# A two-layer graph kernel: the score and value stages of a head pair joined into one stage of 16 steps each, and all adjacency quarters read from memory

## The chip, the core and the metric

The kernel runs on one core of one Trainium2 chip. The metric is the device time of one launch in microseconds (us), as the median of several runs. Everything is computed in 32-bit floats. The engines of the core work side by side, each through its own queue in order: PE (TensorE, matrix products), ACT (ScalarE), DVE (VectorE), POOL (GpSimd), and SP, which here issues nearly all DMA transfers.

## What is computed

There are 16 batch items of 1024 nodes with 256 channels, and one adjacency matrix of 1024 x 1024. Cut to what matters:

```python
# layer 0, on each batch item
c = mean over channels of x                                   # one value per node
A = abs(abs(sigmoid(c_m - c_n) - 0.5) - 0.5) * 2              # 1024 x 1024, symmetric
g = relu((x^T @ (adj * A)) * para)                            # the queries
k, v = split(x @ kv_w)                                        # keys and values, 4 heads of 64
attn = softmax(q @ k^T * scale);  x = layernorm(x + attn @ v)
# layer 1
h = relu(x @ w1_loop + adj @ (x @ w1_neigh) + b1)             # 128 wide
h = relu(h @ w2_loop + adj @ (h @ w2_neigh) + b2)             # 256 wide
x = layernorm(x + (x + h) * 0.5)
```

## The kernel before

All instructions are written out by hand in program order (`tc.manual_schedule()`), and each engine works through its own instructions in that order. The main loop in `run()` goes over the 16 batch items `b`. In iteration `b` the attention of item `b` is computed, the queries, keys and values of item `b + 1` are prepared, and layer 1 of earlier items is done: the first graph product of item `b - 1` (`c1`) and the second of item `b - 2` (`c2`) are joined in `Joined.run`. These two products with the adjacency matrix, of two quarters by two quarters each, are done with seven products of half size instead of eight (`Joined.product`, numbers 1 to 7, in the order 1, 2, 6, 7, 5, 4, 3). Each product reads one half-size matrix: the quarters themselves for 1, 2 and 3, and sums of quarters for 6, 7, 5 and 4. Three quarters (`half_adj`) stay on chip as constants; the fourth and the four sums lie in DRAM (`far_adj`), and `Joined.fetch` reads them as two tiles of 512 KB each.

The attention is done in four units: two head pairs, and for each two halves of 512 queries. `Attention.scores(u)` (L626 to L640) has 8 steps, one per 128 keys. In each, PE computes the scores of both heads of the pair into a PSUM tile of two banks (tag "big", 3 buffers), ACT takes the exponential of 128 x 1024 values (L629), and DVE adds it to a running sum (L633, L635); at the end DVE turns and reduces the sum. `Attention.outputs(u)` (L648, L653) multiplies the values with the 8 exponentials into a PSUM tile of one bank (tag "bank", 2 buffers), and DVE turns the result. `Attention.add` divides and adds into the item's residual.

Between the units stand the functions `gap0` to `gap2`:

- `gap0`, after the value steps of unit 0: `means` sums the channels of the next item on ACT (L262), POOL scales the sums (L263), and SP writes the 1024 values to DRAM (`line`, L265), from where they are read back into all 128 partitions (`c_row`, L270). Between the writing and the reading back SP issues `c2.load_x` (L748) and the transfers of two adjacency sums (L183).
- `gap1`, after unit 1: `c1.inner` (L755), the joined product (L762, L939) with pieces of the next item's queries between its parts, and before it the transfers of two rows of `adj` (L474) and of the other two adjacency sums.
- `gap2`, after unit 2: the end of layer 1 for `c2` (`last`, L823, L825, with the residual on DVE).

After unit 3 follow the queries (L577), the layer norm (`BlockedNorm`) and the keys and values (`KeysValues`) of the next item. Most tiles in SBUF are "row" tiles of 128 x 1024 values (4 KB per partition), 25 buffers shared by all uses; a new tile waits until the one that had its buffer has been used up. A DMA that waits for a buffer or for data holds back all later ones on SP.

In item 0 there is no layer 1 yet, and in item 1 there is only the first product of item 0, done with all eight parts (`GraphConv.first`). Behind the loop the last items are brought to an end.

Of the kernel before, what the change touches and what calls it, by code (L numbers as in the profile page):

```python
# [18 lines left out]
def kernel(  # L19
# [31 lines left out]
    nc = tc.nc  # L51
# [17 lines left out]
    ROWS = 25  # L69
# [95 lines left out]
    for a in range(1, Q):  # L165
# [7 lines left out]
    half_adj = {(0, 0): const.tile([P, TJ, FB], F32, name="adjT_00"),  # L173
                (1, 0): const.tile([P, TJ, FB], F32, name="adjT_10"),
                (1, 1): const.tile([P, TJ, FB], F32, name="adjT_11")}
    far_adj = {n: dram.tile([2, P, N], F32, tag=f"adj_{n}", name=f"adjT_{n}", bufs=1) for n in ("01", 1, 2, 3, 4)}
# [16 lines left out]
    def adj_block(i, j, k, rows01):  # L193
        return of_rows(rows01, k) if (i, j) == (0, 1) else half_adj[i, j][:, k, :]

    def adj_sums(rows01, k):

        w11, w21, w22 = (half_adj[ij][:, k, :] for ij in ((0, 0), (1, 0), (1, 1)))
        w12 = of_rows(rows01, k)
# [404 lines left out]
    class Attention:  # L604
# [6 lines left out]
        def __init__(self, b, xB, qT, kT, v):  # L611
            self.b, self.xB, self.qT, self.kT, self.v = b, xB, qT, kT, v
            self.parts, self.o = {}, {}

            self.rden = small.tile([P, len(UNITS) * FB // S], F32, tag="rden", name=f"rden_{b}", bufs=2)
            self.sums = small.tile([P, NC, NB], F32, tag="sums", name=f"sums_{b}", bufs=2)

        def scores(self, u):

            b, (pair, j) = self.b, UNITS[u]  # L620
            self.pr = []
            for mt in range(NT):
                ps = big_psum(f"s_{b}_{u}_{mt}")
                for s in range(2):
                    rows = slice(s * HD, (s + 1) * HD)
                    nc.tensor.matmul(ps[:, ts(s, FB)], self.kT[rows, pair, ts(mt, P)], self.qT[rows, pair, ts(j, FB)],  # L626
                                     start=True, stop=True)
                pr = row_tile(f"pr_{b}_{u}_{mt}")
                nc.scalar.activation(pr, ps, AF.Exp)  # L629
                self.pr.append(pr)  # L630
                if mt == 1:
                    acc = row_tile(f"acc_{b}_{u}")
                    nc.vector.tensor_add(acc, self.pr[0], pr)  # L633
# [9 lines left out]
        def outputs(self, u):  # L643
            b, (pair, j) = self.b, UNITS[u]
            pav = bank_psum(f"av_{b}_{u}")
            for mt in range(NT):
                for s in range(2):
                    nc.tensor.matmul(pav[s * HD:(s + 1) * HD, :],  # L648
                                     self.v[:, mt, pair * P + s * HD:pair * P + (s + 1) * HD],
                                     self.pr[mt][:, ts(s, FB)], start=(mt == 0), stop=(mt == NT - 1))  # L650
            name = f"o_{b}_{u}"
# [88 lines left out]
    class GraphConv:  # L740
# [29 lines left out]
        def first(self, rows01, between=None):  # L770
            for j in range(NJ):
                ph = half_psum(f"h1_ps_{self.b}_{j}")
                self.loop(ph, j, start=True)
                for mt in range(NT):
                    if (j, mt) == (0, TJ) and between:
                        between()
                    nc.tensor.matmul(ph, self.t1[:, mt, :], adj_block(mt // TJ, j, mt % TJ, rows01),
# [26 lines left out]
        def neighbours(self, j, pu, mts, rows01):  # L804
            for mt in mts:
                nc.tensor.matmul(pu, self.h1[:, ts(mt, P)], adj_block(mt // TJ, j, mt % TJ, rows01),
                                 start=(mt == 0), stop=(mt == NT - 1))

        def second(self, rows01, between=None):

            self.uT = row_tile(f"uT_{self.b}")
            for j in range(NJ):
                pu = half_psum(f"u_ps_{self.b}_{j}")
                self.neighbours(j, pu, range(TJ), rows01)
                if j and between:
                    between()
                self.neighbours(j, pu, range(TJ, NT), rows01)
# [42 lines left out]
        def ending(self, dst, rows01, aside):  # L860
# [40 lines left out]
            self.second(rows01, lambda: (bias(0), bias(1), aside(), bias(2), bias(3), quarter(0)))  # L901
# [5 lines left out]
    class Joined:  # L907
# [27 lines left out]
        def product(self, n, dst, start=False, again=False):  # L935
            w = {1: (0, 0), 2: (1, 0), 3: (1, 1)}.get(n)
            rows = None if w else self.far.pop({4: 4, 5: 1, 6: 2, 7: 3}[n])
            for k in range(TJ):
                nc.tensor.matmul(dst, self.x[n][:, k, :], half_adj[w][:, k, :] if w else of_rows(rows, k),  # L939
# [40 lines left out]
    def run():  # L980
# [32 lines left out]
        rows01 = []  # L1013

        def turn_adj(mts):
            for mt in mts:
                i, k = mt // TJ, mt % TJ
                src = tiles.pop(mt)
                for j in range(NJ):
                    if (i, j, k % 2) == (0, 1, 0):  # L1020
                        rows01.append(row_tile(f"adjT_01_{k // 2}"))
                    nc.vector.transpose(adj_block(i, j, k, rows01), src[:, ts(j, FB)])

        for t in range(NT):
# [3 lines left out]
            if t == 4:  # L1028
# [4 lines left out]
                adj_sums(rows01, 0)  # L1033
# [4 lines left out]
        for b in range(B):  # L1038
# [6 lines left out]
            if c2 and more:  # L1045
                c2.load_h1()

# [5 lines left out]
            def gap0():  # L1053
                row = means(q, xb, str(b + 1))
                if both:
                    c2.load_x()
                    both.fetch(2, 3)
                row()
                ready["xT"] = channel_major(blocked, f"xT_{b + 1}")

# [5 lines left out]
            def gap1():  # L1066
# [3 lines left out]
                if both:  # L1070
                    both.left(nc.gpsimd)
                    both.fetch(1, 4)
                    both.run({1: (lambda: q.left(nc.gpsimd),),
                              2: (lambda: att.add(0, 1),),
                              6: (lambda: q.likeness(0), lambda: c3 and c3.moments()),
                              7: (lambda: q.likeness(TJ),),
                              5: (weigh_first,),
                              4: (lambda: c3 and c3.finish(out[b - 3]),),
                              3: (c1.turn_blocks,)})
                else:  # L1080
                    q.left(nc.gpsimd)
                    for t in (0, TJ):
                        q.likeness(t)
                    store("01", rows01)
                    c1.first(rows01, lambda: (att.add(1), adj_sums(rows01, 1), adj_sums(rows01, 2), weigh_first()))
                    c1.turn_blocks()

            def gap2():
                if both:
                    c2.last()  # L1090
# [185 lines left out]
```

## Time and profile before

| | |
|---|---|
| median of 3 runs | 2150.01 us (2149.88 to 2150.26) |
| profiled execution | span 2148.2 us, 1.8 us under the median |
| granted TensorE clock, mean | 0.998 |
| PE busy | 2136.2 us, 99% |
| DVE busy | 1906.8 us, 89% |
| ACT busy | 1039.8 us, 48% |
| POOL busy | 355.2 us, 17% |
| DMA | 290.73 MB, mean 135 GB/s, queue q1 busy 55.6% of 16 engines' span |
| one iteration (item 7 to item 8, first score to first score) | 924.02 to 1056.17, 132.15 us |

The profile is one execution, not the one that was timed. Busy shares are averages over the span. The ends of matmuls are modelled, so that a busy share of PE says little by itself: the distance from the start of one matmul to the start of the next says more. In a timeline each line merges neighbouring instructions of one kind, with its start, its length and their number (x32: 32 instructions; a 32-bit matmul of 512 columns counts as two). In the DMA queue's timeline the length is the time that SP took to issue, and not the time to landing.

### The profile page before, as it was taken

To read this page: it belongs to the slowest core of one execution; us is meant where nothing else is said; L and a number is where in the kernel's file an instruction comes from. 1 tells how busy PE (TensorE), PEld (TensorE's weight loads), DVE (VectorE), ACT (ScalarE), POOL (GpSimd) and SP (SyncE) were. 2 spreads that over 40 slices of the span, in tenths; PEclk is the share of its full clock that TensorE was granted. 3 is DMA by queue.
4 is the path that set the end of the run, shared out by engine and by line. 5 is a ranking of instruction groups with operands and counts; after the bars stand their busy time and mean duration, and the time that the engine had idled before them with its cause. 6 is when DMAs were issued, how large, how long until landed. Compare 5 with 4: busy or idle time off the path is not lost.

```text
span 2148.2 us, 23745 instructions
## 1 busy us (share of the span) xinstructions
PE 2136.2 (99%) x8360; PEld 1021.5 (48%) x8360; DVE 1906.8 (89%) x2350; ACT 1039.8 (48%) x1374; POOL 355.2 (17%) x201
## 2 busy tenths in 40 slices
PE   9999999999999999999999999999999999999998
PEld 5344444544445444454445444454445444444354
DVE  5999988899999899989999899999999899999964
ACT  5745545545345454445544555345553445545412
POOL 1011120121302113030130301203012130121021
PEclk9999999999999999999999999999999999999999
DMA  9393653736557375573755637565374664744343
GB/s 238 117 147 118 147 157 110 146 117 133 149 137 164 95 134 155 137 172 88 122 163 134 160 89 120 173 128 157 109 115 159 128 157 120 129 134 95 122 137 100
DMA packets 612207, 290.73 MB, mean 135 GB/s; under 512 B 504816, under 2 KB 569712, under 8 KB 612080
## 3 DMA queue, kind: packets, MB, share of 16 engines
q1 hardware_dynamic: 611808, 288.87, 55.6%
q8 instruction: 68, 1.11, 0.2%
q14 instruction: 59, 0.48, 0.1%
q10 hardware_dynamic: 272, 0.26, 0.0%
HBM read 242.35 MB, written 46.72 MB: 135 GB/s over the span
## 4 chain that ended last, share of the span: by engine, by line


## 5 line engine op out<-in xcount | busy, mean ns | idle before, releaser
L629 ACT ACTIVATE pr<-s 128x1024 f32<-128x1024 f32 x512 | 476.1, 1054 | 223.2 <-PE s L626 222.6
L635 DVE TENSOR_TENSOR acc<-acc,pr 128x1024 f32<-128x1024 f32 x384 | 482.9, 1258 | 42.2 <-DVE acc L635 2.8
L626 PE MATMUL s<-qT,kT 64*128 64x512 f32 x2048 | 456.8, 596 | 0.0
L648 PE MATMUL av<-pr,v 128*64 128x512 f32 x2048 | 453.6, 595 | 0.0
L626 PEld LDWEIGHTS s<-qT,kT 64*128 64x128 f32 x2048 | 191.6, 186 | 246.3 <-ACT pr L629 112.8
L648 PEld LDWEIGHTS av<-pr,v 128*64 128x64 f32 x2048 | 141.4, 137 | 298.6 <-issue 283.0
L328 POOL TENSOR_TENSOR rstd<-rstd,neg_half 128x32 f32<-128x32 f32 x16 | 98.9, 6181 | 1102.5 <-DVE rstd L326 1102.5
L490 ACT ACTIVATE wg<-c_row,c_col 128x1024 f32<-128x1024 f32 x128 | 146.1, 1141 | 73.9 <-DVE accB L637 65.7
L496 DVE SCALAR_TENSOR_TENSOR wg<-wg,adj 128x1024 f32<-128x1024 f32 x128 | 150.0, 1210 | 11.9 <-ACT wg L491 11.9
L939 PE MATMUL hu_ps<-adj,R 128*128 128x512 f32 x360 | 158.0, 595 | 0.0
L491 ACT ACTIVATE wg<-wg 128x1024 f32<-128x1024 f32 x128 | 135.3, 1057 | 4.1
L577 PE MATMUL g_ps<-wg,S 128*128 128x512 f32 x224 | 115.5, 597 | 0.0
L577 PE MATMUL g_ps<-T,S 128*128 128x512 f32 x224 | 115.2, 596 | 0.0
L577 PE MATMUL g_ps<-wg,x 128*128 128x512 f32 x224 | 109.0, 599 | 0.0
L939 PE MATMUL hu_ps<-adjT,t 128*128 128x512 f32 x240 | 105.7, 592 | 0.0
L939 PEld LDWEIGHTS hu_ps<-adj,R 128*128 128x128 f32 x360 | 67.3, 190 | 78.9 <-issue 76.3
L633 DVE TENSOR_TENSOR acc<-pr,pr 128x1024 f32<-128x1024 f32 x64 | 77.0, 1203 | 19.7 <-ACT pr L629 19.7
L586 ACT COPY P<-g_ps 128x512 f32<-128x512 f32 x14 | 8.2, 585 | 174.8 <-PE g_ps L577 174.8
L758 ACT COPY t<-t_ps 128x1024 f32<-128x1024 f32 x16 | 16.2, 1013 | 143.9 <-PE t_ps L755 143.9
L637 DVE STREAM_TRANSPOSE accB<-acc 128x1024 f32<-128x1024 f32 x64 | 79.7, 1246 | 2.2
L640 DVE TENSOR_REDUCE den_part<-accB 128x32 f32<-128x1024 f32 x64 | 78.0, 1220 | 2.2
L823 PE MATMUL h_ps<-w2n_sb,uT 128*128 128x256 f32 x240 | 72.7, 385 | 0.0
(204 smaller groups left out, 3022.0 us busy)
## 6 DMA issues: line engine op xcount, KB each, us to landing
adj<-in_adj_dram SPq DMA_DIRECT2D x128, 512.0 KB, 5.1
adj<-adjT SPq DMA_DIRECT2D x120, 512.0 KB, 10.2
para<-in_L_gnn_para_dram SPq DMA_DIRECT2D x32, 512.0 KB, 4.4
xB_a<-in_x_dram SPq DMA_DIRECT2D x128, 128.0 KB, 4.0
x1d<-xB_a SPq DMA_DIRECT2D x128, 128.0 KB, 3.4
x<-x1d SPq DMA_DIRECT2D x16, 1024.0 KB, 16.1
xB<-in_x_dram SPq DMA_DIRECT2D x120, 128.0 KB, 4.4
x<-in_x_dram SPq DMA_DIRECT2D x15, 1024.0 KB, 6.9
```

What stands on the lines that cost most here:

```text
L328: nc.gpsimd.tensor_tensor(self.rstd, self.rstd, neg_half, ALU.pow)
L490: nc.scalar.activation(wg, self.c_row, AF.Abs, bias=self.c_col[:, t:t + 1], scale=-1.0)
L491: nc.scalar.activation(wg, wg, AF.Tanh, scale=-0.5)
L496: nc.vector.scalar_tensor_tensor(wg, wg, 1.0, self.adj.pop(t), op0=ALU.add, op1=ALU.mult)
L577: nc.tensor.matmul(self.p[n], x_n[:, k, :], w_n, start=(k == 0), stop=(k == TJ - 1))
L626: nc.tensor.matmul(ps[:, ts(s, FB)], self.kT[rows, pair, ts(mt, P)], self.qT[rows, pair, ts(j, FB)], start=True, stop=True)
L629: nc.scalar.activation(pr, ps, AF.Exp)
L635: nc.vector.tensor_add(acc, acc, pr)
L637: nc.vector.transpose(accB, acc)
L640: nc.vector.tensor_reduce(self.part[:, u % 2, :], by_node(accB), AX.X, ALU.add)
L648: nc.tensor.matmul(pav[s * HD:(s + 1) * HD, :], self.v[:, mt, pair * P + s * HD:pair * P + (s + 1) * HD], self.pr[mt][:, ts(s, FB)], start ...
L939: nc.tensor.matmul(dst, self.x[n][:, k, :], half_adj[w][:, k, :] if w else of_rows(rows, k), start=(start and k == 0), stop=(k == TJ - 1), ...
```

## The change

It does five things.

1. **Score and value stages.** For b from 2 on, `both_scores(pair)` computes the scores of both query halves of a pair in one go, 16 steps, and `two_units(pair)` then the 16 value steps. Every fourth step (2, 6, 10, 14) uses two one-bank PSUM tiles instead of a big one, and two Exps of half size. The first unit's values go to half of a big PSUM tile, the second unit's to a bank tile; DVE's turning of them (`turn`) is a function of its own, and comes in DVE's order behind all 16 sums of the stage.
2. **Order of the pieces.** `means` and what hangs on it now stand behind `both_scores(0)`, `c2.last()` stands directly behind the joined product, `c1.turn_blocks()` behind that, and the six later rows of `adj` and their weights behind `both_scores(1)`.
3. **Adjacency quarters.** `half_adj` is gone. All four quarters are stored to DRAM in iteration 1, and the three that the joined product uses are read in each joined product, as "00", "10" and "11".
4. **Order of the transfers.** "00" and "10" stand directly behind `line`, then `c2.load_x`, `c_row`, the two rows of `adj`, and 2, 3, 1, 4 and "11".
5. **Row tiles.** 31 buffers instead of 25.

Items 0 and 1 keep their stages of 8 steps. `rows01` becomes `quarters` throughout. The diff, cut to this:

```diff
-    ROWS = 25
+    ROWS = 31
...
-    half_adj = {(0, 0): const.tile([P, TJ, FB], F32, name="adjT_00"),
-                (1, 0): const.tile([P, TJ, FB], F32, name="adjT_10"),
-                (1, 1): const.tile([P, TJ, FB], F32, name="adjT_11")}
-    far_adj = {n: dram.tile([2, P, N], F32, tag=f"adj_{n}", name=f"adjT_{n}", bufs=1) for n in ("01", 1, 2, 3, 4)}
+    QUARTERS = {(0, 0): "00", (0, 1): "01", (1, 0): "10", (1, 1): "11"}
+    far_adj = {n: dram.tile([2, P, N], F32, tag=f"adj_{n}", name=f"adjT_{n}", bufs=1)
...
+    def fetch_quarters(name, ready=None):
+        return {ij: (ready or {}).get(n) or fetch(n, name) for ij, n in QUARTERS.items()}
+
+    def adj_block(i, j, k, quarters):
+        return of_rows(quarters[i, j], k)
+
...
-        def scores(self, u):
+        def scores(self, u, first=None):
 
             b, (pair, j) = self.b, UNITS[u]
-            self.pr = []
+            self.pr[u] = prs = []
             for mt in range(NT):
-                ps = big_psum(f"s_{b}_{u}_{mt}")
+                name = f"s_{b}_{u}_{mt}"
+                split = first is not None and (first + mt) % 4 == 2
+                if split:
+                    halves = [bank_psum(f"{name}_{s}") for s in range(2)]
+                else:
+                    ps = big_psum(name)
+                    halves = [ps[:, ts(s, FB)] for s in range(2)]
                 for s in range(2):
                     rows = slice(s * HD, (s + 1) * HD)
-                    nc.tensor.matmul(ps[:, ts(s, FB)], self.kT[rows, pair, ts(mt, P)], self.qT[rows, pair, ts(j, FB)],
+                    nc.tensor.matmul(halves[s], self.kT[rows, pair, ts(mt, P)], self.qT[rows, pair, ts(j, FB)],
                                      start=True, stop=True)
                 pr = row_tile(f"pr_{b}_{u}_{mt}")
-                nc.scalar.activation(pr, ps, AF.Exp)
-                self.pr.append(pr)
+                if split:
+                    for s in range(2):
+                        nc.scalar.activation(pr[:, ts(s, FB)], halves[s], AF.Exp)
+                else:
+                    nc.scalar.activation(pr, ps, AF.Exp)
+                prs.append(pr)
                 if mt == 1:
                     acc = row_tile(f"acc_{b}_{u}")
-                    nc.vector.tensor_add(acc, self.pr[0], pr)
+                    nc.vector.tensor_add(acc, prs[0], pr)
                 elif mt > 1:
                     nc.vector.tensor_add(acc, acc, pr)
...
+        def both_scores(self, pair):
+            for j in range(NJ):
+                self.scores(NJ * pair + j, j * NT)
+
+        def outputs(self, u, psum_tile=bank_psum, turned=True):
             b, (pair, j) = self.b, UNITS[u]
-            pav = bank_psum(f"av_{b}_{u}")
+            pav = psum_tile(f"av_{b}_{u}")
+            prs = self.pr.pop(u)
             for mt in range(NT):
                 for s in range(2):
                     nc.tensor.matmul(pav[s * HD:(s + 1) * HD, :],
                                      self.v[:, mt, pair * P + s * HD:pair * P + (s + 1) * HD],
-                                     self.pr[mt][:, ts(s, FB)], start=(mt == 0), stop=(mt == NT - 1))
-            name = f"o_{b}_{u}"
+                                     prs[mt][:, ts(s, FB)], start=(mt == 0), stop=(mt == NT - 1))
+            self.o[u] = pav
+            if turned:
+                self.turn(u)
+
+        def turn(self, u):
+            name, pav = f"o_{self.b}_{u}", self.o[u]
             self.o[u] = work.tile([P, FB], F32, tag="o", name=name) if u % 2 else row_tile(name)[:, 0:FB]
             nc.vector.transpose(self.o[u], pav)
...
-            w = {1: (0, 0), 2: (1, 0), 3: (1, 1)}.get(n)
-            rows = None if w else self.far.pop({4: 4, 5: 1, 6: 2, 7: 3}[n])
+            rows = self.far[{1: "00", 2: "10", 3: "11", 4: 4, 5: 1, 6: 2, 7: 3}[n]]
             for k in range(TJ):
-                nc.tensor.matmul(dst, self.x[n][:, k, :], half_adj[w][:, k, :] if w else of_rows(rows, k),
+                nc.tensor.matmul(dst, self.x[n][:, k, :], of_rows(rows, k),
                                  start=(start and k == 0), stop=(k == TJ - 1), skip_group_check=again)
...
-            if c2 and more:
+            if c2:
                 c2.load_h1()
+            if more:
+                q = (FastQueries if c1 else Queries)(b + 1, xb)
 
             def load_next():
                 nonlocal coming
                 if b + 2 < B:
                     coming = load_x(b + 2, str(b + 2)), load_blocked(b + 2, str(b + 2))
 
...
             def weigh_first():
                 q.times_adj(0)
                 q.times_adj(TJ)
                 q.right(0)
 
+            def two_units(pair, before_first=lambda: None, before_second=lambda: None):
+                u = NJ * pair
+                att.outputs(u, half_psum, turned=False)
+                before_first()
+                att.turn(u)
+                att.outputs(u + 1, turned=False)
+                before_second()
+                att.turn(u + 1)
+
...
+            elif more:
+                att.both_scores(0)
+                row = means(q, xb, str(b + 1))
+                both.fetch("00", "10")
+                c2.load_x()
+                row()
+
+                def next_xT():
+                    ready["xT"] = channel_major(blocked, f"xT_{b + 1}")
+
+                two_units(0, before_second=next_xT)
+                kv = KeysValues(b + 1, ready["xT"])
+                kv.sums()
+                for t in (0, TJ):
+                    q.load(t)
+                both.fetch(2, 3, 1, 4, "11")
+                c1.inner()
+                both.left(nc.gpsimd)
+                both.run({1: (lambda: q.left(nc.gpsimd),),
+                          2: (lambda: att.add(0, 1),),
+                          6: (lambda: q.likeness(0), lambda: c3 and c3.moments()),
+                          7: (lambda: q.likeness(TJ),),
+                          5: (weigh_first,),
+                          4: (lambda: c3 and c3.finish(out[b - 3]),)})
+                c2.last()
+                c1.turn_blocks()
+                att.both_scores(1)
+                order = (1, TJ + 1, 2, TJ + 2, 3, TJ + 3)
+                for t in order:
+                    q.load(t)
+                for t in order:
+                    q.likeness(t)
+
+                def weigh_second():
+                    q.times_adj(1)
+                    q.times_adj(TJ + 1)
                     q.right(1)
...
+
+                two_units(1, before_second=weigh_second)
+            else:
+                att.both_scores(0)
+                two_units(0)
+                att.add(0, 1)
+                att.both_scores(1)
+                two_units(1)
...
-                c2.load_h1()
                 c2.load_x()
-                both.fetch(2, 3)
+                both.fetch("00", "10", 2, 3)
                 c1.inner()
                 both.left(nc.gpsimd)
-                both.fetch(1, 4)
-                both.run({1: (lambda: att.add(3), att.watch), 2: (norm.mean, norm.squares, norm.sum_squares), 7: (norm.variance,),
+                both.fetch(1, 4, "11")
+                both.run({1: (lambda: att.add(2, 3), att.watch), 2: (norm.mean, norm.squares, norm.sum_squares), 7: (norm.variance,),
...
-        both.fetch(2, 3, 1, 4)
-        rows01 = fetch("01", "e")
+        both.fetch("00", "10", 2, 3, 1, 4, "11")
+        quarters = fetch_quarters("e", both.far)
```

## Prediction

> **What bounds the kernel now.** I read the busy shares first, then TensorE's timeline over one steady iteration, then ScalarE's and the DMA queue's timelines over the same stretch, then busy times by stretch. The chain of waits is empty on this page, so the bound has to be read from the start times of the matmuls.
>
> The page's busy shares:
>
> ```profile
> PE 2136.2 (99%) x8360; PEld 1021.5 (48%) x8360; DVE 1906.8 (89%) x2350; ACT 1039.8 (48%) x1374; POOL 355.2 (17%) x201
> ```
>
> TensorE's timeline (start us, us, what):
>
> ```profile
> 924.02 7.14 PE L626 MATMUL s<-qT,kT 64*128 64x512 f32 x32
> 931.09 7.09 PE L648 MATMUL av<-pr,v 128*64 128x512 f32 x32
> 938.11 7.14 PE L626 MATMUL s<-qT,kT 64*128 64x512 f32 x32
> 945.17 7.09 PE L648 MATMUL av<-pr,v 128*64 128x512 f32 x32
> 952.19 3.84 PE L755 MATMUL t_ps<-w1n_sb,x1T 128*128 128x128 f32 x32
> 955.87 1.88 PE L762 MATMUL hu_ps<-x1T,w1l_sb 128*128 128x512 f32 x4
> 957.58 7.03 PE L939 MATMUL hu_ps<-adjT,t 128*128 128x512 f32 x16
> 964.45 0.33 PE L662 MATMUL den_ps<-den_part,fold 128*128 128x64 f32 x2
> 964.62 10.52 PE L939 MATMUL hu_ps<-adj,R 128*128 128x512 f32 x24
> ```
>
> 16 matmul rows of 512 columns take 964.45 - 957.58 = 6.87 us, 0.429 us each. A score or value stage is 16 such passes (two 64-wide matmuls side by side), so 6.87 us too; it takes 7.07 and 7.02 us from start to start. Nothing else is lost: TensorE never waits for data here, it pays 0.20 us per score stage and 0.15 us per value stage for changing the tiling of its array. Scores of this batch item start at 924.02, the next item's at 1056.17: 132.15 us per item, all of it matmul time. So the end moves one for one with anything that makes TensorE wait.
>
> **What is removed.** Per joined iteration (b = 2 to 14, 13 of them) four score and four value stages become two and two: 2 x 0.20 + 2 x 0.15 = 0.70 us. The second layer (L823, L825) no longer stands between a value and a score stage: it takes 1004.84 - 997.74 = 7.10 us for 16 pairs spaced 0.43 us (6.9 us), so 0.20 us more. Together 0.90 us; b = 15 saves 0.70. Sum: 13 x 0.90 + 0.7 = **12.4 us gained**, if TensorE stays fed.
>
> **What feeds the score stage.** A score step is 0.86 us on TensorE; ScalarE's Exp is one per 0.92 us (8 in 7.44 us). Steps 2, 6, 10, 14 use the two bank tiles, so every step reuses the buffer of four steps earlier. Exp 11 ends at about 925.20 + 11 x 0.92 + 1.05 = 936.4; step 15 starts at 924.2 + 15 x 0.86 = 937.1: 0.7 us to spare. Two half Exps cost 2 x 0.48 us (L455 to L457, 923.01 to 923.48) against 0.92, or up to 2 x 0.585 (the mean of L586's copies of this shape): 0 to 1.0 us per stage, hidden by that spare up to its 0.7. I take 0. The first value tile now sits in a big buffer that the joined product's third accumulator takes next: VectorE turns it after 16 sums, two transposes and two reductions (2 x 11.6 us from 929.54, so at 953.5); TensorE wants it at 955.5. 2 us to spare, no cost.
>
> **What is moved: the row of means and all transfers behind it.** The means are queued on ScalarE behind 8 Exps today, behind 16 then.
>
> ```profile
> 925.20 7.44 ACT L629 ACTIVATE pr<-s 128x1024 f32<-128x1024 f32 x8 [1.12 <-PE s L626]
> 932.44 0.49 ACT L262 ACTIVATE x<-x 128x256 f32<-128x256 f32 x1
> ...
> 939.28 7.44 ACT L629 ACTIVATE pr<-s 128x1024 f32<-128x1024 f32 x8 [3.50 <-PE s L626]
> ```
>
> They begin at 932.44; then at 925.20 + 12 x 0.92 + 4 x 0.95 = 940.0, 7.5 us later. The DMA of "line" needs them (POOL's c_col), and SP is in order:
>
> ```profile
> 936.17 0.38 SPq L265 DMA_DIRECT2D line<-c_col  x1
> 936.60 0.57 SPq L748 DMA_DIRECT2D x<-x1d  x1
> 937.23 11.02 SPq L183 DMA_DIRECT2D adj<-adjT  x4
> 948.35 0.58 SPq L270 DMA_DIRECT2D c_row<-line  x1
> 949.03 1.06 SPq L474 DMA_DIRECT2D adj<-in_adj_dram  x2
> 952.38 4.16 SPq L183 DMA_DIRECT2D adj<-adjT  x4
> ```
>
> So line goes out at 943.7 instead of 936.17, and everything behind it. What line does to the queue, by stretches (us, busy of PE, PEld, DVE, ACT, POOL, clock, DMA share, GB/s):
>
> ```profile
> 936.00:940.00 4.00, 4.00 (x22) 1.39 (x19) 3.74 (x4) 0.72 (x1) 0.14 (x1) 1.00 0.73 133
> 940.00:948.00 8.00, 8.00 (x40) 3.10 (x38) 7.77 (x7) 6.72 (x8) 2.10 (x1) 1.00 0.54 38
> 948.00:966.00 18.00, 18.00 (x78) 9.46 (x75) 14.53 (x15) 1.60 (x2) 8.70 (x6) 1.00 0.91 356
> ```
>
> After its 1024 writes of 4 bytes almost nothing moves for some 10 us (38 GB/s), then the backlog drains, one 512 KB tile per 1.28 us (time to landing of the tiles of L183). The same read of x, issued with no line ahead in the last iteration, lands in 6.6 us; here in 16.1.
>
> Today the first half of far tile "2", which product 6 reads at 964.62, is issued at 937.23 and lands 16.4 us later, at 953.6: 11 us early. In the change, between line and that tile stand "00" and "10" (4 tiles), x (2 tiles' bytes), c_row, two adjacency rows: 9 tiles' bytes, then it. Today x, four tiles, c_row, two rows, then the first half of "1" are the same bytes in the same queue; that half was issued at 952.38 and landed 11.1 us later, at 963.5: 27.3 us after line. Over the 13 iterations this lies between 26.3 and 29.6. So "2" would land at 943.7 + 27.3 = 971.0. TensorE wants it at 964.62 less the 0.35 us saved on two stages: 964.3. **A wait of 6.7 us**, with product 6 and the whole rest of TensorE's queue behind it. What could shorten it: during the stoppage about 300 packets of 1 KB went through; packets of 4 KB could carry 0.9 MB more, 2.2 us at 410 GB/s. What stopped longest decides a landing, so I take half: 5.6 us; bounds 4.5 and 9 (29.6 us after line). The other tiles follow at 1.28 us, faster than TensorE uses them (1.72 us per tile). "00" (wanted at 957.2) and "10" (960.7) come out of the same queue at about 956 to 960: no further wait.
>
> **After the wait: the array's clock.** At the program's start, out of idleness:
>
> ```profile
> 1.41 3.61 PE L990 MATMUL idle<-ident 128*128 128x128 f32 x16 [1.41 <-POOL ident masks.py:199]
> 4.86 2.60 PE L232 MATMUL xT_ps<-ident,x 128*128 128x128 f32 x16
> ```
>
> 16 transposes take 3.45 us, 0.215 us each; the next 16 of the same shape come at 0.15 us or less ((7.30 - 4.86) / 16). Half speed for 3.45 us is 1.7 us lost. No stretch of this trace shows whether a pause of 6 us brings it back: bounds 0 and 3.4 us per pause (twice that row); I take that row, 1.7. [...] By the rows alone it could also be nothing, which would make the sum 22 us lower.
>
> **The rest.** In the second stage VectorE starts its sums later, behind the second layer's residuals; I put pair(3)'s third difference at 0 to 0.3 us after its product wants it: 0 to 4 us in all, I take 0. Extra bytes: 3 MB in 15 joined products, 45 on 291 MB, in stretches where the queue is idle (966 to 984 moves 1 GB/s): nothing but what is counted. Six extra row tiles replace 24 KB of constant tiles.
>
> **The sum.** 13 x (5.6 + 1.7) = 94.9 us lost, 12.4 gained: 82.5 us. The profiled run spans 2148.2 us, 1.8 under the median; added to the median, 2150.0 + 82.5 = 2232.5, so **2232 us**.
>
> **Rivals.**
> 1. *The streams come in time* (faster): if "2" lands within 20.6 us of line, 13 x 0.90 + 0.7 is all there is: 2137.6 us. For it: today's "2" lands 17.4 us after line. Against it: seven tiles' bytes more stand ahead then. It decides at a landing of 20.6 us; every 1 us beyond is 13 us, so a wait of 0.95 us already eats the gain. 0.18.
> 2. *The wait without a slow clock*: 2150 - 12.4 + 13 x 4.5 to 6.7 = 2196 to 2225. 0.26.
> 3. *Long packets slip through the stoppage, so 1 to 3 us are left*: 2150 - 12.4 + 13 to 39 = 2151 to 2177. 0.10.
> 4. *The change does not do what it says*: scores still come in eights because of buffers taken back late. Then stages still follow each other without a switch, and only ScalarE's lag shows: about no change. 0.04.
>
> **How the numbers follow.** The forecast has 0.42; its own range is 2196 to 2277 (13 x (7.0 + 3.4 + 0.3) - 12.4 = 127 above). Slower by over 0.2% (about what a measurement of this kernel can tell from no change, 4.3 us): 0.42 + 0.26 + 0.10 = 0.78; within it 0.04; faster 0.18. The range for 8 in 10 leaves out rival 1 alone: 2150 to 2277.
>
> **What would show it.** Right: in each of 13 iterations one gap on TensorE of 4 to 9 us before L939's first "adj,R" product, ended by DMA adj<-adjT; line issued some 19.7 us after the item's first score; "2" landing 24 to 30 us after line; matmuls after the gap spaced 0.86 us for a while; six switches of tiling per item. Wrong: no gap there and 131.25 us per item (rival 1), or a gap that ends at ScalarE's Exp or VectorE's turning instead.

## The result, and the profile after

The changed kernel takes 2256.2 us (2255.96 to 2259.01) against 2150.0 us: a ratio of 1.0497, 95% interval 1.0482 to 1.0511. It is 106 us slower; the forecast was 82 us slower, 2232 us, with 2277 as the upper end. The profiled execution spans 2254.2 us, 106.0 us more than the one of before.

The busy shares of the page, and the groups of products, with the idle time before them after the bar:

```profile
PE 2160.5 (96%) x8356; PEld 1038.2 (46%) x8356; DVE 1895.1 (84%) x2346; ACT 1046.6 (46%) x1486; POOL 342.0 (15%) x201
...
L959 PE MATMUL hu_ps<-adj,R 128*128 128x512 f32 x480 | 239.9, 658 | 66.3 <-DMA adj<-adjT 66.3
```

TensorE was 99% busy and is 96% busy now, and nearly all of its new idle time stands before one line. L959 is what L939 was. TensorE's timeline over the item that starts at 963.11 us shows where:

```profile
963.11 14.00 PE L633 MATMUL s<-qT,kT 64*128 64x512 f32 x64
977.04 13.95 PE L664 MATMUL av<-pr,v 128*64 128x512 f32 x64
...
997.91 7.10 PE L959 MATMUL hu_ps<-adj,t 128*128 128x512 f32 x16 [1.43 <-DVE K L387]
1004.85 0.33 PE L683 MATMUL den_ps<-den_part,fold 128*128 128x64 f32 x2
1010.85 11.32 PE L959 MATMUL hu_ps<-adj,R 128*128 128x512 f32 x19 [5.67 <-DMA adj<-adjT]
```

The two joined stages run without a gap: 977.04 - 963.11 = 13.93 us for 32 passes of 0.429 (13.74), and 13.88 us for the value stage. Then there are two gaps. Product 1 starts 34.8 us after the item's first score instead of 33.2 (in this item the profile puts the wait down to VectorE's K; the first half of "00" landed at 997.77, 0.14 us before the start, so I read it as that transfer). Product 6 starts only when the first half of "2" is there. Its 19 passes shown take 11.32 us, where 24 took 10.52 before.

The DMA queue's timeline over the same item:

```profile
983.37 0.38 SPq L266 DMA_DIRECT2D line<-c_col  x1
983.80 2.00 SPq L182 DMA_DIRECT2D adj<-adjT  x4
985.85 0.73 SPq L769 DMA_DIRECT2D x<-x1d  x1
995.52 2.53 SPq L271 DMA_DIRECT2D c_row<-line  x1
998.15 1.29 SPq L475 DMA_DIRECT2D adj<-in_adj_dram  x2
999.58 11.52 SPq L182 DMA_DIRECT2D adj<-adjT  x9
```

The order is the one of the diff, and c_row goes out only when line has landed. The stretches behind line (us, busy of PE, PEld, DVE, ACT, POOL, clock, DMA share, GB/s) repeat the stoppage and the backlog of before:

```profile
983.00:987.00 4.00, 4.00 (x22) 1.33 (x20) 3.69 (x4) 0.00 (x0) 0.35 (x1) 1.00 0.12 1
987.00:995.00 8.00, 8.00 (x53) 4.98 (x50) 7.72 (x8) 0.20 (x1) 1.99 (x1) 1.00 0.25 27
995.00:1012.00 17.00, 9.90 (x24) 4.38 (x23) 14.38 (x21) 1.40 (x2) 10.33 (x7) 0.94 1.00 375
```

27 GB/s while line's writes run, 375 GB/s afterwards; and a granted clock of 0.94 in the stretch that holds the pause. TensorE's waits over the whole run (us in total, times, longest), where before had none beyond the 1.4 us at the program's start:

```profile
PE hu_ps L959 <- DMA adj<-adjT: 75.9, 24, 5.7
...
PE sum_ps L253 <- DVE rden_min L702: 1.9, 1, 1.9
PE den_ps L683 <- DVE den_part L651: 1.5, 1, 1.5
```

From the start times of the matmuls, summed over the 13 joined items (each term is what the distance between two starts exceeds its usual value by):

| | per item | in all |
|---|---|---|
| product 1 waits for "00" | 0.6 to 1.6 us | 14.5 |
| product 6 waits for the first half of "2" | 4.83 to 5.83 us | 68.4 |
| passes at half speed behind that pause, 0.854 us apart | 1.6 to 3.1 us | 28.2 |
| last step of the queries waits for VectorE's T (L552) | 0.24 us | 3.2 |
| item 15: fold sum of the layer norm 2.0, division of units 0 and 1 1.65 | | 3.7 |
| tiling switches saved | -0.90 us | -12.4 |
| sum | | 105.6 |

That is 105.6 of the 106.0 us between the spans, but two rows are off by about 1 us each way. From first score to first score the 13 items are 103.9 us longer together, where their rows give 102.6; from the first score of item 15 to the end the run is 1.9 us longer, where its rows give 3.0 (3.7 less the 0.7 saved).

### The profile page after: what moved, and what is told of

The parts are those of the page before. It is cut to its first block, busy times and chain, and to the rows that moved or that the text cites. A ratio compares the mean times of both kernels' runs of the same rounds, so it can differ in the third digit from the quotient of the medians.

```text
span 2254.2 us, 23956 instructions
## 1 busy us (share of the span) xinstructions
PE 2160.5 (96%) x8356; PEld 1038.2 (46%) x8356; DVE 1895.1 (84%) x2346; ACT 1046.6 (46%) x1486; POOL 342.0 (15%) x201
## 4 chain that ended last, share of the span: by engine, by line
## 5 line engine op out<-in xcount | busy, mean ns | idle before, releaser
L640 ACT ACTIVATE pr<-s 128x1024 f32<-128x1024 f32 x400 | 396.6, 1111 | 145.3 <-PE s L633 145.3
L633 PE MATMUL s<-qT,kT 64*128 64x512 f32 x2048 | 449.2, 593 | 0.0
L664 PE MATMUL av<-pr,v 128*64 128x512 f32 x2048 | 447.4, 594 | 0.0
L959 PE MATMUL hu_ps<-adj,R 128*128 128x512 f32 x480 | 239.9, 658 | 66.3 <-DMA adj<-adjT 66.3
L959 PEld LDWEIGHTS hu_ps<-adj,R 128*128 128x128 f32 x480 | 100.8, 214 | 192.2 <-issue 191.8
L491 ACT ACTIVATE wg<-c_row,c_col 128x1024 f32<-128x1024 f32 x128 | 146.1, 1141 | 85.7 <-DVE den_part L651 65.8
L638 ACT ACTIVATE pr<-s 128x512 f32<-128x512 f32 x224 | 133.0, 703 | 0.0
L959 PE MATMUL hu_ps<-adj,t 128*128 128x512 f32 x240 | 106.9, 597 | 12.4 <-DMA adj<-adjT 9.6
L851 DVE TENSOR_TENSOR z<-h_ps,b_sb 128x1024 f32<-128x1024 f32 x30 | 36.7, 1225 | 89.0 <-PE h_ps L846 89.0
L981 ACT COPY snap<-hu_ps 128x512 f32<-128x512 f32 x15 | 8.8, 585 | 187.4 <-PE hu_ps L959 187.4
```

The lines of the kernel that those rows point to most:

```text
L491: nc.scalar.activation(wg, self.c_row, AF.Abs, bias=self.c_col[:, t:t + 1], scale=-1.0)
L633: nc.tensor.matmul(halves[s], self.kT[rows, pair, ts(mt, P)], self.qT[rows, pair, ts(j, FB)], start=True, stop=True)
L638: nc.scalar.activation(pr[:, ts(s, FB)], halves[s], AF.Exp)
L664: nc.tensor.matmul(pav[s * HD:(s + 1) * HD, :], self.v[:, mt, pair * P + s * HD:pair * P + (s + 1) * HD], prs[mt][:, ts(s, FB)], start=(mt ...
L959: nc.tensor.matmul(dst, self.x[n][:, k, :], of_rows(rows, k), start=(start and k == 0), stop=(k == TJ - 1), skip_group_check=again)
```

## Experiments

The theory: line's 1024 writes of 4 bytes stop the queue, the transfers behind them come out in order, 1.28 us per half tile, and the change puts line 7.5 us later and more in front of "2". Rivals: the stages of 16 steps or the streamed bytes cost the time themselves. Before took 2149.97 to 2150.45 us beside these runs.

**Stages of 16 steps with three quarters on chip.** The quarters on chip leave room for 25 row tiles only, as before.

```diff
-    ROWS = 31
+    ROWS = 25
...
-    QUARTERS = {(0, 0): "00", (0, 1): "01", (1, 0): "10", (1, 1): "11"}
+    half_adj = {(0, 0): const.tile(...), (1, 0): const.tile(...), (1, 1): const.tile(...)}
...
-                both.fetch("00", "10")
                 c2.load_x()
-                row()
...
+                both.fetch(2, 3)
+                row()
...
-                both.fetch(2, 3, 1, 4, "11")
+                both.fetch(1, 4)
```

> Stages joined as in the change, but the three quarters stay on chip (25 row tiles); behind line stand x, tiles 2 and 3, c_row, two rows of adj, 1 and 4. Theory (a late line and four tiles more ahead of tile 2, together, make TensorE wait): line goes out 20.3 us after the item's first score, tile 2 lands 17 to 20.6 us after line (as before the change), product 6 wants it 20.0 us after line, so almost no wait: 2150 - 12.4 + 3.2 (a 0.24 us wait at the end of the queries) + 3.7 (item 15) = 2145 us, at most 2150. Rival (the 16-step stage itself starves TensorE, through ScalarE or VectorE): over 2200 us, as in the change.

Measured: 2226.5 us (2220.3 to 2230.7), ratio 1.0357 (1.034 to 1.0373). A miss. The wait of product 6 is gone (0.5 us in one item; products wait 7.2 us in all), but the score stage now has one of its own. TensorE's waits, ScalarE's timeline and TensorE's timeline in one item:

```profile
PE s L632 <- ACT pr L637: 33.6, 13, 2.9
```

```profile
1034.62 1.08 ACT L637 ACTIVATE pr<-s 128x512 f32<-128x512 f32 x2 [3.62 <-issue]
```

```profile
1020.43 12.29 PE L632 MATMUL s<-qT,kT 64*128 64x512 f32 x56
1035.27 2.53 PE L632 MATMUL s<-qT,kT 64*128 64x512 f32 x8 [2.55 <-ACT pr L637]
```

Fourteen of the 16 steps run through; then ScalarE stands 3.62 us although its scores are there, and TensorE behind it; in nine items the granted clock falls to half behind that (its mean over the run is 0.990). All this is in the second score stage of the item. The prediction had passed over this: 16 exponentials alive at once, the running sum and the second stage's tiles do not fit into 25 row tiles. That is a reading: the profile names no tile that ScalarE waits for. Two runs further down bear on it.

**Stages of 8 steps with streamed quarters.** The other half alone: the loop of before, with 31 row tiles, all quarters from DRAM, and the change's order of transfers. The order of transfers, as a diff against the kernel of before:

```diff
-                c2.load_x()
-                both.fetch(2, 3)
+                both.fetch("00", "10")
+                c2.load_x()
...
-                both.fetch(1, 4)
+                both.fetch(2, 3, 1, 4, "11")
```

> Stages of 8 steps in the order of before, but all quarters are read from memory (31 row tiles, transfers in the order of the change). Theory: line goes out 12.2 us after the first score, tile 2 lands 26.3 to 29.6 us after it, wanted at 28.4: 2150 to 2153 us, with a wait in one iteration or two. Rival (the 45 MB more of traffic cost by themselves, or row tiles come free too late): 2190 us or more.

Measured: 2150.65 us (2150.2 to 2152.56), ratio 1.0003 (0.9994 to 1.0012). Every item takes 132.15 us, as before. The first half of "2" lands 25.0 to 27.8 us after line here too, but line goes out 7.6 us sooner in the item. So the bytes (341 MB against 291) cost nothing, and neither does the order of the transfers alone; what costs is that order together with a later line.

**Line in pieces of 32 bytes.** The change, with line written so that each partition's 8 means lie together: 128 pieces in place of 1024 single values. The row is read back as before, so the means stand in another order and the weights of the adjacency are those of other nodes; the amount of work is the same.

```diff
-        nc.sync.dma_start(out=line.rearrange("o (t p) -> p (o t)", p=P), in_=c_col)
+        nc.sync.dma_start(out=line.rearrange("o (p t) -> p (o t)", p=P), in_=c_col)
```

> The change, with line written as 128 pieces of 32 bytes instead of 1024 of 4 bytes (the means then stand in another order, so the weights of the adjacency are those of other nodes). Theory (the small writes stop the queue for some 10 us): line lands within 3 to 4 us, tile 2 about 15 to 18 us after line, before it is wanted: 2145 us, no slow matmuls. Rival (the stoppage is that of the reads behind line, or just volume): tile 2 still 25 us or more after line and 2240 to 2260 us.

Measured: 2145.15 us (2143.7 to 2145.95), ratio 0.9975 (0.9964 to 0.9986). The queue's timeline and TensorE's in one item:

```profile
941.76 0.34 SPq L266 DMA_DIRECT2D line<-c_col  x1
942.16 1.85 SPq L182 DMA_DIRECT2D adj<-adjT  x4
```

```profile
954.71 7.03 PE L959 MATMUL hu_ps<-adj,t 128*128 128x512 f32 x16
961.58 0.33 PE L683 MATMUL den_ps<-den_part,fold 128*128 128x64 f32 x2
961.74 10.52 PE L959 MATMUL hu_ps<-adj,R 128*128 128x512 f32 x24
```

On average line lands 1.45 us after its issue (11.2 us in the change), and the first half of "00" 4.3 us after that issue (14.0); the first half of "2" takes 16.3 to 18.0 us (25.8 to 27.3). Both gaps are gone, and the 24 passes of products 6, 7 and 5 take 10.52 us again. Line is issued no sooner than in the change (20.2 us after the first score). One line of code turns the change from 5% slower into 0.25% faster: the stoppage is line's 4-byte writes, not the volume behind them. The same 4 KB lands in 1.45 us as pieces of 32 bytes and in 11.2 us as pieces of 4. Whether the number or the size of the pieces makes it, these two runs do not tell.

**Useless products in the gap.** Six products of 512 columns ahead of product 6 in the 13 joined items; they fill 5.2 us of its pause and are overwritten.

```diff
             turn_to(2)
+            if c1.b < B - 2:
+                for _ in range(6):
+                    nc.tensor.matmul(second, ident, self.far["10"][0][:, 0:FB], start=True, stop=True)
             self.product(6, first, again=True)
```

> The change, with 6 matmuls of 512 columns (12 passes, 5.15 us) of no use queued in front of product 6 in items 2 to 14, written to an accumulator that product 7 starts afresh. Theory (the pause of 5.3 us brings the array's half clock, 2.2 us lost each): the pause is filled, no matmul runs at half speed, 2256 - 28 + 2 = 2230 us. Rival (the slow matmuls behind the pause are slow for the tiles that still land then): they stay slow, 2256 us or up to 3 us more.

Measured: 2241.0 us (2238.7 to 2246.0), ratio 1.043 (1.0415 to 1.0446). TensorE's timeline in one item:

```profile
993.09 7.11 PE L959 MATMUL hu_ps<-adj,t 128*128 128x512 f32 x16 [1.56 <-DMA adj<-adjT]
...
1000.20 5.37 PE L982 MATMUL hu_ps<-adj,ident 128*128 128x512 f32 x12
1005.41 10.46 PE L959 MATMUL hu_ps<-adj,R 128*128 128x512 f32 x24
```

No pass behind the fillers is slow: 24 take 10.46 us. So the slow passes come from the pause and not from the tiles. The gain was 15 us and not the 26 expected, since the landings were later in this run (product 1 waited 1.5 us on average instead of 1.1, and in some items product 6 still waited behind the fillers).

**Transfers in the order of need.** 2 and 3 directly behind "00" and "10", x last.

```diff
-                both.fetch("00", "10")
-                c2.load_x()
+                both.fetch("00", "10", 2, 3)
...
-                both.fetch(2, 3, 1, 4, "11")
+                both.fetch(1, 4, "11")
+                c2.load_x()
```

> The change with one thing different: behind line the transfers stand in the order in which TensorE asks for them (00, 10, 2, 3, then c_row and the two adjacency rows, then 1, 4, 11, and x last). Theory (line's 4-byte writes stop the queue and the backlog comes out in order, a 512 KB half tile per 1.28 us): the first half of 2 now stands behind four half tiles instead of nine tiles' bytes, so it lands some 19.5 us after line, where 20.0 are there: no wait at product 6 and no slow clock behind it. Product 1 still waits for 00, which lands 14.4 us after line: 1.1 to 1.5 us per item. Sum: 2150 - 12.4 + 13 x 1.2 + 3.2 (queries' tail) + 3.7 (last item) = 2160, 2157 to 2165. Rival (the far tiles are late because of the bytes asked for in all, whatever their order, or because SP issues them late): product 6 still waits 3 us or more, 2200 or above.

Measured: 2157.9 us (2156.5 to 2160.6), ratio 1.004 (1.0026 to 1.0054). Product 1 waits 0.5 us on average and product 6 no more than that (0.58 late against the ideal); an item takes 132.48 us, and the clock stays up (0.998 in the mean). Nothing but the order of eight transfers is worth 98 us here. An item still takes 1.0 us more than the 131.49 of the run with 32-byte pieces. Some 0.6 of it stand ahead of product 6, since "00" is the first in the queue behind line; the rest, mostly in three items, lies behind product 6 and was not followed up.

**Transfers ahead of line.** "00", "10" and 2 asked for before the item's scores.

```diff
+                both.fetch("00", "10", 2)
                 att.both_scores(0)
                 row = means(q, xb, str(b + 1))
-                both.fetch("00", "10")
                 c2.load_x()
...
-                both.fetch(2, 3, 1, 4, "11")
+                both.fetch(3, 1, 4, "11")
```

> The change with 00, 10 and 2 asked for ahead of the item's scores, and so ahead of line; 3, 1, 4 and 11 stay behind it. Theory (only the tiles queued behind line's writes are late): these six half tiles land early in the score stage, and the first half of 3, with four half tiles fewer ahead of it, lands some 22.2 us after line, where product 7 wants it 23.5 after: no wait in the joined product, no slow clock. 2150 - 12.4 + 3.2 + 3.7 = 2144.5 (2143 to 2147), as with 32-byte pieces of line. Rival (six row tiles held 20 us longer starve the score stage, as in the version with 25 row tiles, or SP waits for their buffers and sends line later): waits of ScalarE's Exp for a row tile or of product 1, 1 us or more per item, 2157 or above.

Measured: 2147.05 us (2145.85 to 2149.04), ratio 0.9986 (0.9977 to 0.9995). Twelve of the 13 items have no wait (131.5 to 131.85 us); item 2 takes 133.5, and there the rival, a wait for a row tile, may be at work. TensorE's waits in that item:

```profile
PE hu_ps L959 <- ACT t L779: 1.8, 1, 1.8
```

ScalarE's copy of t ran 2.4 us later there than in the run with 32-byte pieces; what it waited for was VectorE's last use of a tile, which I read as the row tile that it needed.

**The two small waits taken out.** The version above, with

```diff
-            for n in (1, 6, 2, 7, 4, 5, 3) if k == TJ - 1 else (1, 2, 3, 5, 7, 6, 4):
+            for n in (1, 2, 6, 7, 4, 5, 3) if k == TJ - 1 else (1, 2, 3, 5, 7, 6, 4):
...
                 two_units(0)
-                att.add(0, 1)
                 att.both_scores(1)
+                att.add(0, 1)
```

> The kernel of the run above with the two small waits taken out that the changed kernel has and the prediction did not: the last step of the queries goes through its products as 1, 2, 6, 7, 4, 5, 3 instead of 1, 6, 2, 7, 4, 5, 3, so that those of the second weights come later, and in the last item the division for units 0 and 1 stands behind the second score stage. Theory: 13 x 0.24 and 1.65 us go, 2144.5 - 3.1 - 1.6 = 2139.8 (2138.5 to 2142). If these waits only move on, 2144 to 2145.

Measured: 2142.9 us (2142.2 to 2144.8), ratio 0.9968 (0.9956 to 0.998), the lowest median of all, though the next version's 2143.5 us is not told apart from it. From item 3 on, items take 131.25 to 131.37 us: the 0.90 us under 132.15 that the prediction read from the tiling switches. Of the 3 us above the expectation, 2.1 are item 2's again, which the expectation had left out, and 0.6 a wait at the division in the last item. Moving the division gained nothing: from the first score of item 15 to its first layer-1 matmul (L776) it takes 57.7 us now and 57.6 in the version above. Of the 5.4 us between the two profiles, 3.4 are the queries' wait and small ones in the items, 0.2 are item 2's, and most of the rest are slow passes in the last item that only the profile above has.

**The same without early fetches, but line in pieces of 32 bytes.**

```diff
-        nc.sync.dma_start(out=line.rearrange("o (t p) -> p (o t)", p=P), in_=c_col)
+        nc.sync.dma_start(out=line.rearrange("o (p t) -> p (o t)", p=P), in_=c_col)
...
-            q.c_row = work.tile(...)
-            nc.sync.dma_start(out=q.c_row, in_=line.to_broadcast([P, N]))
+            c_row = work.tile(...)
+            nc.sync.dma_start(out=c_row, in_=line.to_broadcast([P, N]))
+            q.c_row = c_row.rearrange("q (p t) -> q t p", p=P)
...
-            nc.scalar.activation(wg, self.c_row, AF.Abs, ...)
+            nc.scalar.activation(wg.rearrange("q (t p) -> q t p", p=P), self.c_row, AF.Abs, ...)
...
```

> The change with the fetches left where the change put them, line written as 128 pieces of 32 bytes, and the same two small waits taken out. The means keep their order here: the row is read back as it lies and ScalarE's Abs reads it with a stride of 32 bytes (and in the other order for the first item). Theory: as in the run with the early fetches, 2139.8 (2138.5 to 2142); ScalarE has the room for the strided Abs even if it takes 0.3 us more each. Rival (the strided reading costs ScalarE so much that its Exps of the second stage come late): over 2145, with Abs of 2 us or more.

Measured: 2143.5 us (2142.0 to 2144.3), ratio 0.9968 (0.9956 to 0.9981). All 13 items are free of waits. ScalarE's Abs with the stride, by line (times, busy in all, mean ns), is nearly twice as long as the 1141 ns that it took without:

```profile
L492 ACT ACTIVATE wg<-c_row,c_col 128x1024 f32<-128x1024 f32 x128 | 269.9, 2109 | 57.9 <-DVE den_part L652 38.5 <-PE av L665 19.3
```

In the joined items ScalarE has that room; item 0 became 2.3 us longer by a wait for an Exp. Another 1.6 us are slow passes in the last item, told of below.

**Early fetches from item 3 on.** To free item 2 of its wait, it fetches "00", "10", 2 and 3 behind line, ahead of x.

```diff
-                both.fetch("00", "10", 2)
+                early = b > 2
+                if early:
+                    both.fetch("00", "10", 2)
                 att.both_scores(0)
                 row = means(q, xb, str(b + 1))
+                if not early:
+                    both.fetch("00", "10", 2, 3)
...
-                both.fetch(3, 1, 4, "11")
+                both.fetch(*((3,) if early else ()), 1, 4, "11")
```

> The version with early fetches and the two small waits taken out, but in item 2, where the first copy of t on ScalarE waited 1.8 us for a row tile, 00, 10, 2 and 3 are asked for behind line. Theory: 2142.9 - 2.0 = 2140.9 (2139.5 to 2142.5). If item 2 then waits for 00 as other items did in that order: 2141 to 2143.

Measured: 2148.95 us (2146.2 to 2151.3), ratio 0.9991 (0.9982 to 1.0). A miss: item 2 now takes 137.3 us. TensorE's timeline in it:

```profile
315.14 5.37 PE L959 MATMUL hu_ps<-adj,R 128*128 128x512 f32 x8 [2.90 <-ACT wg L491]
```

The row of means came out behind eight half tiles and x at 311.17 us; ScalarE's Abs waited for it, and the copy of a finished product stood behind that Abs on ScalarE. After 2.9 us TensorE's next 8 passes took 5.37 us instead of 3.6. Of the 6.8 us between this profile and that of the version with all early fetches, 4.0 are item 2's and 2.1 lie in the last item, most of them its slow passes.

**The same with x last in item 2.**

```diff
-                c2.load_x()
+                if early:
+                    c2.load_x()
                 row()
...
+                if not early:
+                    c2.load_x()
```

> The version with early fetches from item 3 on, but in item 2 with x moved behind all other transfers. In the version before it, item 2's row of means (c_row) came out of the queue behind the tiles 2 and 3 and x, 311.17 us into the run, and ScalarE's first Abs of it, with the copy of the second product behind it, made TensorE wait 2.9 us and run slowly after that. Theory: c_row lands about 4 us sooner (307), product 7 does not wait, item 2 takes 131.3 to 132.3 us instead of 137.3, and the whole 2140.9 (2139.5 to 2143). Rival (the 3 us are those of a row tile and only move to another product): item 2 stays above 134, 2144 or more.

Measured: 2144.0 us (2142.9 to 2146.1), ratio 0.9972 (0.9963 to 0.9982). Item 2 takes 133.0 us, so the 4 us of the run before were the late row of means. The rest is product 1's wait for "00" in item 2 (1.1 us), and slow passes in the last item (1.8 us) that the profile of the version with all early fetches does not have. Without them the two profiles would be level (2142.9 - 1.8 = 2141.1 us and 2141.0), so neither is shown to be the better one.

**28 and 26 row tiles.** The version "early fetches from item 3 on", with nothing else changed.

```diff
-    ROWS = 31
+    ROWS = 28
```

> The kernel of the run above with 28 row tiles instead of 31, nothing else. Theory (the score stages of 16 steps need the six more row tiles; the version with 25 lost its time to them): waits of ScalarE's Exp for a row tile appear, and the time lies between 2145 and 2190. Rival (the 25 row tiles had nothing to do with that loss; it came from the order of transfers there): 2141, no such waits.

> The same with 26 row tiles. Theory: more of the same waits, 2190 to 2240, as the version with 25 row tiles had (2226). Rival: 2141.

Measured: 2198.1 us (2194.0 to 2200.6), ratio 1.0215 (1.02 to 1.0231) with 28, and 2278.6 us (2274.5 to 2283.5), ratio 1.0598 (1.0582 to 1.0615) with 26. More than expected of both: 49 us for three tiles and another 80 for the next two. ScalarE's waits with 28:

```profile
ACT pr L640 <- DVE accB L648: 36.3, 12, 3.1
```

Exp number 14 of the first stage waits 3 us for the tile that VectorE gives back when it has turned the first sum; line goes out at 24.3 us instead of 20.3. SP's transfers into row tiles are late as well, and TensorE waits 38.0 us in 14 times for them. With 26, product 1 starts 6.4 to 7.2 us later in the item from item 3 on. There the scores themselves wait 67.3 us in 26 times for ScalarE's Exps. So a lack of row tiles delays line and the transfers first, and then starves the 16-step stages. That the 25 tiles cost the first experiment its time is likely and not shown by itself: there ScalarE stood in the second score stage and here, with 28, in the first, and here the streamed quarters and the early fetches take row tiles too. The streaming of the quarters costs nothing by itself and frees the room for the tiles.

## Why the prediction was right, point by point

- **The tiling switches, 12.4 us gained.** Right. 131.25 us per item in the versions without waits against 132.15.
- **The score stage fed, the split Exps free, the first value tile turned in time.** Right: 13.93 and 13.88 us per stage. But the row tiles, to which the prediction gave one short sentence, carry this: with 26 of them, in the version with early fetches, it fails.
- **Line at 19.7 us after the first score.** 20.23 us. The step to ScalarE's means held (15.86 us measured, 15.98 worked out). POOL's scaling behind it was read from one item, 0.28 us; over the run its median was 0.745 us in before and 0.837 in after. That one row was no fair sample.
- **"2" lands 27.3 us after line, less 1.1 for the longer packets.** 26.4 us (25.8 to 27.3), where the tenth transfer of before had a mean of 27.6. The credit of 1.1 came out at about the right size, but by luck: it was given for longer packets that carry more through the stoppage, and less went through. Between line's issue and its landing 0.18 to 0.34 MB were moved beside it in the change, 0.39 to 1.31 MB in before. What was smaller is the sum of bytes from line's issue to the landing in question, 5.6 to 6.1 MB against 6.1 to 7.1.
- **The wait, 5.6 us at product 6; none for "00".** Together 6.4 us: 1.1 at product 1 and 5.3 at product 6. The wait at product 1 doesn't add to the other one; product 6 starts when its tile lands, at 46.7 us after the first score, whatever was lost before. The sum needed 6.47 us (46.72 - 40.25), mostly because line was 0.5 us later. "00" was put at 956 at the earliest against a want of 957.2, and that margin was thinner than the spread of the landings. Short: 13 x 0.8, some 10.5 us.
- **The half clock, 1.7 us per pause.** Right that it comes: the granted clock is 0.50 behind the pause, and with the fillers in it no pass is slow (24 in 10.46 us). The size was 2.17 us (1.6 to 3.1). Short: 6 us. The row at the program's start (1.7, from 0.215 us for each transpose where eight from 12.45 us on take 0.11 each) was nearer than zero, and the bounds, 0 and twice that row, hold all 13.
- **The queries' tail, 0 to 0.3 us, taken 0.** 0.24 us, 3.2 in all: the upper bound was the better value, since VectorE is late in every item alike.
- **Item 15** was counted as 0.7 us gained only. Its two waits make 3.7 us, though the run's end came only 1.9 us later by it, the 0.7 gained included. My reading, not tested: with no next item, nothing stands between the last stages, and VectorE's two turnings and divisions came together.
- **Bytes cost nothing.** Right (stages of 8 steps, streamed).

10.5 + 6 + 3.2 + 3.7 = 23.4 of the 24 us between forecast and result, with the 1 us each way said above. The upper end of the range, 2277, was not the sum of the prediction's own bounds: it took a wait of 7.0 us, where the bound was 9, which gives 2303; the measured 6.4 lies within either. Of the rivals, the first (streams in time) is what the change does once line is written in larger pieces; the forecast's case won, with every lost term on the low side.

## What to carry to other kernels

When a piece of work is moved, follow the first transfer that depends on it, and then everything queued behind that transfer: here a row of 1024 values was moved by 7.7 us and held back nine tiles' bytes, of which only c_row needed it, and TensorE behind them. Ask for data that depends on nothing ahead of a transfer of many tiny pieces, or make the pieces larger (here 1.45 us to land instead of 11.2). Price a pause of the matrix engine as the pause and the slow passes that can follow it (here 5.3 and 2.2 us), and take margins of less than the spread of the landings as gone.

## What of the hardware was not expected

- A transfer of 1024 pieces of 4 bytes took 9.6 to 12.1 us to land in the change and let 1 to 27 GB/s through beside it in the item shown above; the same 4 KB in 128 pieces of 32 bytes landed in 1.4 to 1.8 us (once 2.3 in the second version with them).
- The half clock does not follow the length of the pause alone. Pauses of 0.6 to 1.6 us were never followed by slow passes in the change. Pauses of 4.8 to 5.8 us always were, by 4 to 7 passes of 0.854 us. The pause of 2.03 us in the last item stands in twelve profiles; six of them, the change and the version with the lowest median among them, show no slow pass behind it, and six show 4 or 5 (1.6 to 1.8 us, in both versions with 32-byte pieces for one).
- The granted clock in the trace of the change is 0.50 from 1009.91 to 1016.74 us in the item shown above, and 1.00 on both sides. It falls once in each of the 13 joined items, for 6.83 us in twelve of them and for 3.41 us in one, and the times of all these changes lie whole multiples of 3.413 us apart, within 0.002. Cut at these multiples, 13 stretches of the run between 20 and 2240 us end in a fall; TensorE's passes, 0.429 us each from their start, fill 0.00 to 0.33 of them. None of the other stretches at full clock is filled less than 0.41. That one holds the pause of 2.03 us in the last item, and the clock stays up behind it.
- ScalarE's Abs of 128 x 1024 values took 2.11 us with reads 32 bytes apart, and 1.14 us with them side by side.
